# Text scores in half-row groups: two 64-row products at once instead of 128-row products over masked keys

## The chip, the cores and the metric

The kernel runs on one core of a Trainium2 chip. The metric is the device time of one execution in microseconds (µs). Three runs of the kernel before gave 744.82, 745.06 and 745.11, so the median is 745.06. The core has a tensor engine (PE, with its weight loads shown as a row of their own, PEld), a vector engine (DVE), a scalar engine (ACT), a general engine (POOL) and a queue (SP) that issues most transfers. Products are made in single precision; each product shows as two matmul instructions in the profile, each with a weight load.

## The reference

The block is a cross attention with a second, "adapter" attention beside it. Only the first part is touched by the change in the main loop, but both share the tensor engine.

```
query = hidden @ Wq                      # hidden: 2 x 2048 x 640, 8 heads of 80
keyt  = enc @ Wk ; valt = enc @ Wv       # enc: 2 x 124 text tokens x 384
hs    = mha(query, keyt, valt)           # softmax over the 124 tokens, head by head
ca_q1 = einsum('btc,th->bch', ca, Wq_ca)[:, indices]   # 4 adapter tokens
ca_hs1 = mha(ca_q1, hidden, hidden)      # 2048 keys
ca_hs2 = mha(ca_hs1 @ Wq, ca @ Wk_ca, ca @ Wv_ca)
out = (hs + ca_hs2) @ Wout + b_out + hidden
```

## The kernel before, in words

The 2 x 2048 rows are cut into 32 tiles of 128 rows, 16 for each of the two batch entries. Four tiles make a block of 512 rows, for which the queries are made; two tiles make a unit, for which the values and the output are made.

**Features.** Two heads have 160 features together, so a group of two heads does not fit 128 partitions. The kernel keeps queries and keys, both with features on partitions, as five chunks: chunks 0 to 3 hold the first 128 features of each pair of heads (80 of the even head, 48 of the odd one), and chunk 4 holds the remaining 32 of each of the four pairs. `columns` (L390) cuts the columns of a weight matrix this way, for `wq_sb` and for the keys' weights.

**Keys.** `setup_keys` (L584) makes the keys of the text, a chunk at a time (`pk`), and writes them to `kpad`, multiplied by a mask. Each of chunks 0 to 3 is written twice, once with only the even head's features left and once with only the odd head's (`side`); chunk 4 is written four times, once for each pair (`quarter`).

**Scores.** `scores` (L971) makes the text scores of two tiles. For a tile and for each half `u` of the heads (four heads) it takes one PSUM bank `sc` and makes three products over 128 rows, with 248 columns each: two chunks of two heads, and chunk 4 for the two odd heads. DVE takes the maximum of each row and head (`m<-sc`) and subtracts it (`p<-sc`). After each half there is a `yield`, at which other work can be put. When both halves are done, ACT takes the exponential, DVE the sum and its reciprocal, POOL the division (`divided`), DVE turns the result (`eb`), which then goes through memory (`kept`) and comes back as `pT`, with tokens on partitions.

**Values and output.** `values` makes the products `ph` (tokens to features), and `po` (with `Wout`), and DVE adds `po` to the rows.

**The adapter.** Its steps are a main line in the program, twice, once for each batch entry: `maxima` (products `s` of 32 rows with 512 columns, four at once, and a DVE maximum of 2048 elements), `less_maxima` (`pm`), and `contraction` (`s` with 384 columns, ACT's exponential, and `acc`). `yz_block` (`pyz`) and `y_rows` (`pt_y`) prepare their operands. `setup_a2` prepares the adapter's first weights, out of `k2`, `blk["k"]` and the turned `Wq`; `groups_turned` (L464) turns `k2` so that its features lie on partitions.

**Order.** The order of the tensor engine is written out by the program: `TensorInOrder` adds up an estimated time of each product, and `weave` and `Mix` put text work (queries, scores, values) into gaps of the adapter's main line by that estimate. `together` and `beside` take one step of each of several generators in turn, from `yield` to `yield`. The SP queue also keeps the program's order. Other engines take their instructions in the order that the tile framework gives them.

**PSUM.** There are eight banks. The adapter's `s` has four (`sq`) and `acc` one (`ps_a`). Text products take turns in the three of `ps_m`, in the maxima of the second batch entry with `ps_a` as a fourth; only when the adapter is through do they have all eight. A product that takes a bank waits until the reader of the bank's last product is done.

Of the kernel before, what the change touches and what calls it, by code (L numbers as in the profile page):

```python
# [8 lines left out]
F32 = mybir.dt.float32  # L9
# [4 lines left out]
P = 128  # L14
HEADS = 8
T = 4
# [161 lines left out]
def kernel(  # L178
# [129 lines left out]
    band(side2, [[-VH, 2]], VH)  # L308
    eighth = const.tile([P, HEADS], F32, name="eighth")
    band(eighth, [[-VR, HEADS]], VR)  # L310
    s2f = const.tile([P, NCC, HEADS, T], F32, name="s2f")
    nc.gpsimd.memset(s2f, 0.0)

# [7 lines left out]
    wyz4 = const.tile([P, B, 4, G], F32, name="wyz4")  # L321
    nc.gpsimd.memset(wyz, 0.0)
    nc.gpsimd.memset(wyz4, 0.0)
    kpad = const.tile([P, B, 3 * 4, NK], F32, name="kpad")

    vpad = [const.tile([P, HEADS, VH + 2 * VR], F32, name=f"vpad_{b}") for b in range(B)]
    y_sb = const.tile([P, NST, HEADS, G], F32, name="y_sb")
# [61 lines left out]

    def columns(t, last):  # L390

        dve.tensor_copy(
            last.rearrange("p n (g d) -> p n g d", g=4),
            t.rearrange("p n (g d) -> p n g d", g=4)[:, :, :, P:],
        )
        return lambda i, c: t[:, i, D2 * c : D2 * c + P] if c < 4 else last[:, i, :]

    ctxT = sp.tile([P, NCC, B, NTOK], F32, name="ctxT")

# [61 lines left out]
                )  # L461
        return pg

    def groups_turned(name, t, n):  # L464

        pt = mm_tile(name)
        transpose(pt[:, :P], t[:, :P], ident)
        for g in range(4):
            matmul(
                pt[R * g : R * (g + 1), P : P + n], t[:, P:], ident[:, G * g : G * g + n],  # L470
                start=True, stop=True, skip_group_check=True,
            )
        return pt[:, :P].rearrange("p (c k) -> p c k", c=4), pt[:, P : P + n]

    def by_blocks(name, *products):

# [13 lines left out]
    def setup_a2():  # L490

        pg = by_groups("p2_kca", cadT, w_c["kca"])
        k2 = sp.tile([P, D2], F32, name="k2")
        evacuate(k2, pg[:, :D2])
        yield 2.0
        load_w("vca", Wv_ca)

        wqT = []
        for i in range(NCH):
            if i < 4:  # L500
                t = xrow.tile([P, H], F32, tag="x", name=f"wqT_{i}")
            else:
                t = sp.tile([P, H], F32, name=f"wqT_{i}")
            wqT.append(t.rearrange("p (c s) -> p c s", c=NCH))
            for c0, c1 in ((0, 4), (4, NCH)):
                pt = mm_tile(f"pt_wq_{i}_{c0}")
                for c in range(c0, c1):
                    transpose(pt[:, (c - c0) * P : (c - c0 + 1) * P], wq_of(i, c), ident)
                evacuate(
                    wqT[i][:, c0:c1], pt[:, : (c1 - c0) * P].rearrange("p (c s) -> p c s", s=P)  # L510
                )
            yield 1.5
            if i == 0:
                most, rest = groups_turned("pt_k2", k2, B * T1)
                for j in range(2):
                    k0 = T1 * j
                    dve.tensor_scalar(
                        blk["k"][:, 0, :, : B * 2 * T1].rearrange("p c (b k) -> p c b k", b=B)[
                            :, :, :, k0 : k0 + T1
                        ],  # L520
                        most[:, :, : B * T1].rearrange("p c (b t) -> p c b t", b=B),
                        side[:, j : j + 1], None, ALU.mult,
                    )
                dve.tensor_tensor(
                    blk["k"][:, 1, :, : B * 2 * T1].rearrange("p c (b k) -> p c b k", b=B)[
                        :, :, :, T1:
                    ],
                    rest.rearrange("p (x b t) -> p x b t", x=1, b=B).to_broadcast([P, 4, B, T1]),
                    quarter.rearrange("p (g x y) -> p g x y", x=1, y=1).to_broadcast(
                        [P, 4, B, T1]  # L530
                    ),
                    ALU.mult,
                )
                yield 1.5
        a2 = sp.tile([P, NCH * P], F32, name="a2")
        pa = [mm_tile("pa2_0", ps_a), mm_tile("pa2_1")]
        by_blocks(
            "k",
            *[(pa[i // 4][:, i % 4 * P : (i % 4 + 1) * P], lambda c, t=wqT[i]: t[:, c], i % 4 == 0)
              for i in range(NCH)],  # L540
        )
        nc.scalar.copy(a2[:, : 4 * P], pa[0])
        dve.tensor_copy(a2[:, 4 * P :], pa[1][:, :P])
        yield 1.5
        for c0, c1 in ((0, 4), (4, NCH)):
# [38 lines left out]
    def setup_keys():  # L584


        load_w("v", Wv)
        k_of = columns(w_c["k"], sp.tile([P, NCC, P], F32, tag="w4", name="k4"))
        for c in range(NCH):
            pk = mm_tile(f"pk_{c}")  # L590
            for cc in range(NCC):
                matmul(
                    pk[:, : B * NTOK],
                    k_of(cc, c),
                    ctxT[:, cc, :, :].rearrange("p b t -> p (b t)"),
                    start=(cc == 0),
                    stop=(cc == NCC - 1),
                )
            pk3 = pk[:, : B * NTOK].rearrange("p (b t) -> p b t", b=B)[:, :, :NK]
            for i in range(2 if c < 4 else 4):  # L600
                of = side[:, i : i + 1] if c < 4 else quarter[:, i : i + 1]
                dve.tensor_scalar(kpad[:, :, 2 * c + i, :], pk3, of, None, ALU.mult)
            yield
        setup_rows()

# [11 lines left out]
    def setup_values():  # L617
# [21 lines left out]
        for j in range(2):  # L639
# [8 lines left out]
        for b in range(B):  # L648
            n = 2 * T
            dve.tensor_tensor(  # L650
                blk["v"][:, 1, :, n * b : n * (b + 1)].rearrange("p g (j t) -> p g j t", j=2),
                rest[:, T * b : T * (b + 1)].rearrange("p (x y t) -> p x y t", x=1, y=1).to_broadcast(
                    [P, 4, 2, T]
                ),
                eighth.rearrange("p (g j x) -> p g j x", g=4, x=1).to_broadcast([P, 4, 2, T]),
                ALU.mult,
            )
        yield
        for b in range(B):
            nc.gpsimd.memset(vpad[b], 0.0)  # L660
# [310 lines left out]
    def scores(m):  # L971

        q = q_of[m // 2]
        before = None
        for b, st in tiles(m):
            rows = slice(st % 4 * P, (st % 4 + 1) * P)
            e = pools["e"].tile([P, HEADS, NTOK], F32, tag="e", name=f"p_{b}_{st}")
            for u in range(2):
                sc = mm_tile(f"sc_{b}_{st}_{u}")
                for i, c in enumerate((2 * u, 2 * u + 1, 4)):  # L980
                    to = sc[:, : 4 * NK].rearrange("p (i j k) -> p i j k", i=2, j=2)
                    n0 = 2 * c if c < 4 else 2 * (4 + u)
                    matmul(
                        to[:, i, :, :] if c < 4 else to[:, :, 1, :],
                        q[:, c, rows],
                        kpad[:, b, n0 : n0 + 2, :],
                        start=(i == 0),
                        stop=(i == 2),
                        skip_group_check=True,
                    )  # L990
                s4 = sc[:, : 4 * NK].rearrange("p (h k) -> p h k", k=NK)
                m = small.tile([P, 4], F32, tag="m", name=f"m_{b}_{st}_{u}")
                dve.tensor_reduce(m, s4, AX.X, ALU.max)
                dve.tensor_tensor(
                    e[:, 4 * u : 4 * u + 4, :NK], s4,
                    m.unsqueeze(2).to_broadcast([P, 4, NK]), ALU.subtract,
                )
                yield
            nc.scalar.activation(e[:, :, :NK], e[:, :, :NK], AF.Exp, scale=SCALE)  # L999
            nc.gpsimd.memset(e[:, :, NK:], 0.0)  # L1000
            if before is not None:
                divided(*before)
            before = b, st, e
        yield
        divided(*before)
# [343 lines left out]
```

## Time and profile before

| | |
|---|---|
| median of three runs | 745.06 µs (744.82 to 745.11) |
| the profiled execution, first to last instruction | 747.5 µs |
| PE busy | 728.9 µs, 98% |
| DVE busy | 372.4 µs, 50% |
| ACT busy | 197.3 µs, 26% |
| POOL busy | 133.4 µs, 18% |
| granted clock of PE | 1.000 of full speed |

The span of the profiled execution is all the time that the profile tells of it, and is 2.4 µs above the median of the runs. In a group of instructions a form such as 64*128 says how many rows and columns of the tensor engine's array an instruction takes, and 64x512 how many partitions and columns its moving operand has. Busy time is a union: products overlap in the engine, so the time that a product adds is read from the distance between starts of what follows it, not from its own duration.

### The profile page before, as it was taken

The page shows a single profiled execution, that of the slowest core. Times are in us where ns is not written, and L with a number is a line of the kernel's source. Part 1 is how long each engine was busy: PE and PEld are TensorE (multiplying, and loading weights), DVE is VectorE, ACT ScalarE, POOL GpSimd, SP SyncE. Part 2 cuts the span into 40 slices and gives each one's busy share as a digit, 9 for nine tenths or more (in the row PEclk, how much of TensorE's full clock was granted, in tenths as well). Part 3 has the DMA queues.
Part 4 walks back from the last instruction along what each step waited for, and adds up shares of the span by engine and source line. Part 5 has one row for each costly group of instructions (what it writes and reads, how often), then busy time and mean ns, then how long its engine had stood idle before and what let it go on. Part 6 is the DMA issues. An engine that isn't in the chain of part 4 may idle for free.

```text
span 747.5 us, 9397 instructions
## 1 busy us (share of the span) xinstructions
PE 728.9 (98%) x3809; PEld 373.7 (50%) x3809; DVE 372.4 (50%) x500; ACT 197.3 (26%) x246; POOL 133.4 (18%) x184
## 2 busy tenths in 40 slices
PE   6989999999999999999999999999999999999998
PEld 4553443343345455555545454534443556566765
DVE  2046747553164446677768585411340546345631
ACT  2221122024444443212011110443534411011100
POOL 7000000002021012316220220010010012631330
PEclk9999999999999999999999999999999999999999
DMA  9909070005623968499998295410920426985883
GB/s 286 178 3 157 1 71 1 0 1 152 66 92 74 182 115 190 117 260 211 245 177 216 36 191 116 134 33 14 187 54 18 127 92 198 232 218 152 219 241 96
DMA packets 147429, 96.28 MB, mean 129 GB/s; under 512 B 118133, under 2 KB 118965, under 8 KB 145338
## 3 DMA queue, kind: packets, MB, share of 16 engines
q1 hardware_dynamic: 142266, 85.10, 48.1%
q0 software_dynamic: 5120, 10.59, 8.0%
q8 instruction: 30, 0.49, 0.3%
q14 instruction: 13, 0.11, 0.1%
HBM read 63.81 MB, written 31.85 MB: 128 GB/s over the span
## 4 chain that ended last, share of the span: by engine, by line
PE 91%; DVE 4%; DMA 2%; issue 1%; ACT 1%; POOL 0%; SPq 0%; DVEq 0%; ACTq 0%; POOLq 0%
PE pq L28 24%; PE po L28 23%; PE s L28 13%; PE sc L28 11%; PE acc L28 6%; PE ph L28 6%; PE pyz L28 3%; DMA pT<-kept 1%; PE pk L28 1%; PE pv L28 1%; PE pt_y L41 1%; DMA xz<-in_x_dram 1%; ACT ea L856 1%; DVE xt L55 1%; DVE p L55 1%
## 5 line engine op out<-in xcount | busy, mean ns | idle before, releaser
L28 PE MATMUL po<-wout_sb,hsT 128*128 128x320 f32 x640 | 186.5, 438 | 0.6 <-DVE xo L55 0.6
L28 PE MATMUL pq<-xt,wq_sb 128*128 128x512 f32 x320 | 153.7, 612 | 0.0
L28 PEld LDWEIGHTS po<-wout_sb,hsT 128*128 128x128 f32 x640 | 118.5, 190 | 69.6 <-issue 25.1
L55 DVE TENSOR_REDUCE mx<-s 128x4 f32<-128x2048 f32 x48 | 109.9, 2290 | 66.1 <-PE s L28 66.1
L856 ACT ACTIVATE ea<-s 128x1536 f32<-128x1536 f32 x64 | 92.7, 1449 | 106.1 <-PE s L28 106.0
L1014 POOL TENSOR_TENSOR p<-p,r 128x992 f32<-128x992 f32 x32 | 61.6, 1984 | 262.4 <-DVE r L55 262.4
L55 DVE TENSOR_TENSOR xo<-xo,po 128x320 f32<-128x320 f32 x64 | 30.9, 483 | 140.8 <-PE po L28 140.8
L28 PEld LDWEIGHTS pq<-xt,wq_sb 128*128 128x128 f32 x320 | 58.1, 192 | 75.7 <-issue 70.2
L28 PE MATMUL sc<-kpad,q 128*128 128x248 f32 x384 | 94.1, 384 | 0.9 <-DVE p L55 0.9
L28 PEld LDWEIGHTS sc<-kpad,q 128*128 128x128 f32 x384 | 69.2, 189 | 33.7 <-issue 18.5
L55 DVE TENSOR_REDUCE m<-sc 128x4 f32<-128x496 f32 x64 | 42.4, 667 | 62.2 <-PE sc L28 62.2
L272 ACT COPY q<-pq 128x512 f32<-128x512 f32 x31 | 18.2, 586 | 171.0 <-PE pq L28 171.0
L28 PE MATMUL s<-ca,yz 32*128 32x384 f32 x512 | 59.4, 533 | 2.3 <-ACT ea L856 2.3
L999 ACT ACTIVATE p<-p 128x992 f32<-128x992 f32 x32 | 33.0, 1030 | 92.3 <-DVE p L55 92.3
L28 PE MATMUL s<-yz,ca 32*128 32x512 f32 x384 | 54.7, 640 | 1.8 <-DVE mx L55 1.0
L28 PE MATMUL acc<-ea,y_sb 128*32 128x384 f32 x512 | 54.5, 498 | 1.6 <-ACT ea L856 1.6
L1109 POOL DMA_INDIRECT xo<-o,query x24 | 37.4, 1558 | 99.3 <-DMA xo<-in_x_dram 50.7
L28 PE MATMUL ph<-pT,vpad 128*32 128x256 f32 (+1 forms) x512 | 50.0, 387 | 0.2 <-DMA pT<-kept 0.2
L55 DVE TENSOR_TENSOR p<-sc,m 128x496 f32<-128x496 f32 x64 | 42.6, 671 | 1.7
L55 DVE STREAM_TRANSPOSE eb<-p 128x1024 f32<-128x1024 f32 x32 | 38.1, 1223 | 3.6 <-POOL p L1014 3.6
L28 PE MATMUL pq<-xt,wq 128*128 128x512 f32 x80 | 38.3, 603 | 0.0
L55 DVE TENSOR_REDUCE r<-p 128x8 f32<-128x992 f32 (+1 forms) x34 | 37.7, 1111 | 0.0
(142 smaller groups left out, 393.8 us busy)
## 6 DMA issues: line engine op xcount, KB each, us to landing
kept<-eb SPq DMA_DIRECT2D x16, 1024.0 KB, 5.4
pT<-kept SPq DMA_DIRECT2D x64, 256.0 KB, 5.7
xi<-in_x_dram SPq DMA_DIRECT2D x44, 256.0 KB, 5.2
xo<-in_x_dram SPq DMA_DIRECT2D x32, 320.0 KB, 5.3
out_dram<-xo SPq DMA_DIRECT2D x22, 320.0 KB, 2.2
xi<-in_x_dram SPq DMA_DIRECT2D x44, 64.0 KB, 4.2
early<-xo SPq DMA_DIRECT2D x8, 320.0 KB, 2.6
xe<-early SPq DMA_DIRECT2D x8, 320.0 KB, 5.5
```

Source lines behind the costliest of these rows:

```text
L28: ins = self.tc.nc.tensor.matmul(out, lhsT, rhs, **kw)
L41: ins = self.tc.nc.tensor.transpose(out, in_, ident)
L55: self.last = getattr(self.tc.nc.vector, name)(*args, **kw).ins
L272: nc.scalar.copy(dst, src)
L856: nc.scalar.activation(e, q4[:, :, :CAD], AF.Exp, scale=SCALE)
L999: nc.scalar.activation(e[:, :, :NK], e[:, :, :NK], AF.Exp, scale=SCALE)
L1014: nc.gpsimd.tensor_tensor(et, et, r.unsqueeze(2).to_broadcast([P, HEADS, NK]), ALU.mult)
L1109: nc.gpsimd.indirect_dma_start(out=t, out_offset=None, in_=o2_of[b], in_offset=bass.IndirectOffsetOnAxis(ap=query[:, st : st + 1], axis=0) ...
```

## The change

The five chunks are cut anew. Chunk `c` of 0 to 3 now holds the last 64 features of the even head on partitions 0 to 63 and the first 64 of the odd head on partitions 64 to 127; chunk 4 holds, on each half, the remaining 16 features of the four even or of the four odd heads. Keys of chunks 0 to 3 are copied as they are (`kmain`), and those of chunk 4 are written four times with a mask (`krest`, `fourth`).

A tile now takes both banks at once. For each of the four pairs there are two products over 64 rows and 124 columns, one on each half of the partitions and into a bank of its own; then two over 64 rows and 496 columns for the remaining features. Even heads end in one bank, odd heads in the other. There is one `yield` for a tile where there were two. The maxima and differences are the same four DVE instructions per tile. `k2` and its turning follow the new chunks: the transposed remainder is now one product with a spread copy (`wide`) and a folded unit matrix (`fold`), and the masks are written by `spread_rest`, whose lines stood in `setup_values` before.

```diff
+    fourth = const.tile([P, 4], F32, name="fourth")
+    nc.gpsimd.tensor_tensor(fourth, eighth[:, :4], eighth[:, 4:], ALU.add)
...
-    kpad = const.tile([P, B, 3 * 4, NK], F32, name="kpad")
+    kmain = const.tile([P, B, 4, NK], F32, name="kmain")
+    krest = const.tile([P, B, 4, NK], F32, name="krest")
...
     def columns(t, last):
 
-        dve.tensor_copy(
-            last.rearrange("p n (g d) -> p n g d", g=4),
-            t.rearrange("p n (g d) -> p n g d", g=4)[:, :, :, P:],
-        )
-        return lambda i, c: t[:, i, D2 * c : D2 * c + P] if c < 4 else last[:, i, :]
+        pairs = t.rearrange("p n (g d) -> p n g d", g=4)
+        rest = last.rearrange("p n (j g d) -> p n j g d", g=4, j=2)
+        dve.tensor_copy(rest[:, :, 0], pairs[:, :, :, :VR])
+        dve.tensor_copy(rest[:, :, 1], pairs[:, :, :, VR + P :])
+        return lambda i, c: t[:, i, D2 * c + VR : D2 * c + VR + P] if c < 4 else last[:, i, :]
...
-    def groups_turned(name, t, n):
+    def groups_turned(name, t, n, apart=False):
 
         pt = mm_tile(name)
         transpose(pt[:, :P], t[:, :P], ident)
-        for g in range(4):
+        if apart:
+            wide = sp.tile([P, 2, 4, VR], F32, name="wide")
+            dve.tensor_tensor(
+                wide, t[:, P:].rearrange("p (j x d) -> p j x d", j=2, x=1).to_broadcast([P, 2, 4, VR]),
+                quarter.rearrange("p (y g x) -> p y g x", y=1, x=1).to_broadcast([P, 2, 4, VR]),
+                ALU.mult,
+            )
+            fold = sp.tile([P, G], F32, name="fold")
+            dve.tensor_reduce(fold, ident.rearrange("p (g k) -> p k g", k=G), AX.X, ALU.add)
+            matmul(
+                pt[:, P : P + n], wide.rearrange("p j g d -> p (j g d)"), fold[:, :n],
+                start=True, stop=True, skip_group_check=True,
+            )
+        for g in range(0 if apart else 4):
...
-        evacuate(k2, pg[:, :D2])
+        evacuate(k2[:, :P], pg[:, VR : VR + P])
+        evacuate(k2[:, P : P + VR], pg[:, :VR])
+        evacuate(k2[:, P + VR :], pg[:, VR + P : D2])
...
-            for i in range(2 if c < 4 else 4):
-                of = side[:, i : i + 1] if c < 4 else quarter[:, i : i + 1]
-                dve.tensor_scalar(kpad[:, :, 2 * c + i, :], pk3, of, None, ALU.mult)
+            if c < 4:
+                dve.tensor_copy(kmain[:, :, c, :], pk3)
+            for i in range(4 if c == 4 else 0):
+                of = fourth[:, i : i + 1]
+                dve.tensor_scalar(krest[:, :, i, :], pk3, of, None, ALU.mult)
...
+            sc = [mm_tile(f"sc_{b}_{st}_{u}") for u in range(2)]
+            for j in range(4):
+                for u in range(2):
+                    half = slice(VH * u, VH * (u + 1))
+                    matmul(
+                        sc[u][:, j * NK : (j + 1) * NK], q[half, j, rows], kmain[half, b, j, :],
+                        start=(j == 0), stop=False, skip_group_check=True,
+                    )
             for u in range(2):
-                sc = mm_tile(f"sc_{b}_{st}_{u}")
-                for i, c in enumerate((2 * u, 2 * u + 1, 4)):
...
+                half = slice(VH * u, VH * (u + 1))
+                matmul(
+                    sc[u][:, : 4 * NK], q[half, 4, rows],
+                    krest[half, b].rearrange("p j k -> p (j k)"),
+                    start=False, stop=True, skip_group_check=True,
+                )
+            for u in range(2):
+                s4 = sc[u][:, : 4 * NK].rearrange("p (h k) -> p h k", k=NK)
                 m = small.tile([P, 4], F32, tag="m", name=f"m_{b}_{st}_{u}")
                 dve.tensor_reduce(m, s4, AX.X, ALU.max)
                 dve.tensor_tensor(
-                    e[:, 4 * u : 4 * u + 4, :NK], s4,
+                    e.rearrange("p (j u) k -> p j u k", u=2)[:, :, u, :NK], s4,
                     m.unsqueeze(2).to_broadcast([P, 4, NK]), ALU.subtract,
                 )
-                yield
+            yield
```

More of the change, by code (lines that the diff above doesn't have):

```diff
@@ L473, in groups_turned, with spread_rest @@
         return pt[:, :P].rearrange("p (c k) -> p c k", c=4), pt[:, P : P + n]
+    def spread_rest(to, rest, t, own):
+        for b in range(B):
+            n = 2 * t
+            dve.tensor_tensor(
+                to[:, 1, :, n * b : n * (b + 1)].rearrange("p g (j t) -> p g j t", j=2),
+                rest[:, t * b : t * (b + 1)].rearrange("p (x y t) -> p x y t", x=1, y=1).to_broadcast(
+                    [P, 4, 2, t]
+                ),
+                own.to_broadcast([P, 4, 2, t]),
+                ALU.mult,
+            )
     def by_blocks(name, *products):
@@ L513, in setup_a2 @@
             if i == 0:
-                most, rest = groups_turned("pt_k2", k2, B * T1)
+                most, rest = groups_turned("pt_k2", k2, B * T1, True)
                 for j in range(2):
@@ L521, in setup_a2 @@
                         most[:, :, : B * T1].rearrange("p c (b t) -> p c b t", b=B),
-                        side[:, j : j + 1], None, ALU.mult,
+                        side2[:, j : j + 1], None, ALU.mult,
                     )
[L524 to L533, printed above, removed]
+                spread_rest(blk["k"], rest, T1, eighth.rearrange("p (j g x) -> p g j x", g=4, x=1))
                 yield 1.5
@@ L647, in setup_values @@
             )
[L648 to L657, printed above, removed]
+        spread_rest(blk["v"], rest, T, eighth.rearrange("p (g j x) -> p g j x", g=4, x=1))
         yield
@@ L977, in scores @@
             e = pools["e"].tile([P, HEADS, NTOK], F32, tag="e", name=f"p_{b}_{st}")
-            for u in range(2):
-                sc = mm_tile(f"sc_{b}_{st}_{u}")
-                for i, c in enumerate((2 * u, 2 * u + 1, 4)):
[L981 to L991, printed above, removed]
+            sc = [mm_tile(f"sc_{b}_{st}_{u}") for u in range(2)]
[6 more added lines that the diff above has]
+                    )
+            for u in range(2):
+                half = slice(VH * u, VH * (u + 1))
[3 more added lines that the diff above has]
+                    start=False, stop=True, skip_group_check=True,
+                )
+            for u in range(2):
+                s4 = sc[u][:, : 4 * NK].rearrange("p (h k) -> p h k", k=NK)
                 m = small.tile([P, 4], F32, tag="m", name=f"m_{b}_{st}_{u}")
```

## The prediction

> **What bounds the kernel now.** I read the busy times first, then the engines by stretch, the costliest groups, the order of time on PE, and the chain that ended last.
>
> The page and the view by stretches (columns: length, then PE, PEld, DVE, ACT and POOL busy with instructions in brackets):
>
> ```profile
> PE 728.9 (98%) x3809; PEld 373.7 (50%) x3809; DVE 372.4 (50%) x500; ACT 197.3 (26%) x246; POOL 133.4 (18%) x184
> 15.00:55.00 40.00, 37.90 (x201) 20.75 (x203) 9.91 (x29) 8.51 (x19) 0.00 (x0) 1.00 0.53 118
> 290.00:430.00 140.00, 138.56 (x666) 74.63 (x666) 100.80 (x118) 28.34 (x47) 39.21 (x34) 1.00 0.78 180
> 600.00:747.00 147.00, 143.89 (x639) 92.60 (x637) 66.60 (x107) 17.65 (x28) 44.31 (x34) 1.00 0.67 181
> PE 91%; DVE 4%; DMA 2%; issue 1%; ACT 1%; POOL 0%; SPq 0%; DVEq 0%; ACTq 0%; POOLq 0%
> ```
>
> PE is busy in every stretch, at a granted clock of 1.00, and 91% of the chain that ended last is PE. DVE comes nearest to it in one stretch, with 100.8 of 140. So time taken off PE comes off the span, until a wait takes its place.
>
> The groups, every shape apart (busy, mean ns of one, idle before):
>
> ```profile
> L28 PE MATMUL sc<-kpad,q 128*128 128x248 f32 x384 | 94.1, 384 | 0.9 <-DVE p L55 0.9
> L55 DVE TENSOR_TENSOR p<-sc,m 128x496 f32<-128x496 f32 x64 | 42.6, 671 | 1.7
> L55 DVE TENSOR_REDUCE m<-sc 128x4 f32<-128x496 f32 x64 | 42.4, 667 | 62.2 <-PE sc L28 62.2
> L28 PE MATMUL pyz<-xt,wyz 64*128 64x512 f32 x32 | 9.0, 641 | 0.0
> L28 PEld LDWEIGHTS pyz<-xt,wyz 64*128 64x128 f32 x32 | 2.4, 184 | 6.5 <-issue 6.5
> L55 DVE TENSOR_SCALAR kpad<-pk,side 128x248 f32<-128x248 f32 x8 | 3.4, 472 | 15.1 <-PE pk L28 15.1
> ```
>
> The scores are 384 instructions, 12 a tile. The fourth line is the form that the change brings, with 512 columns: two products, one on each half of the rows, as in the changed scores. 32 of them fill 9.0 µs, 0.28 each, though one lasts 0.64.
>
> The order of time on PE (start, length, instruction, count); starts are subtracted below:
>
> ```profile
> 49.17 0.71 PE L41 MATMUL pt_a<-ident,a 128*128 128x128 f32 x5
> 49.71 1.02 PE L28 MATMUL pq<-xt,wq 128*128 128x512 f32 x2
> ...
> 62.80 1.14 PE L28 MATMUL s<-yz,ca 32*128 32x512 f32 x8
> 63.87 2.84 PE L28 MATMUL pq<-xt,wq_sb 128*128 128x512 f32 x6
> 66.64 1.14 PE L28 MATMUL s<-yz,ca 32*128 32x512 f32 x8
> ...
> 673.74 4.46 PE L28 MATMUL pq<-xt,wq 128*128 128x512 f32 x10
> 678.03 2.89 PE L28 MATMUL sc<-kpad,q 128*128 128x248 f32 x12
> 680.85 2.95 PE L28 MATMUL ph<-pT,vpad 128*64 128x256 f32 x32
> 683.73 2.78 PE L28 MATMUL sc<-kpad,q 128*128 128x248 f32 x12
> 686.35 3.93 PE L28 MATMUL po<-wout_sb,hsT 128*128 128x320 f32 x14
> ```
>
> Four prices come from it. **A column:** ten instructions of 512 columns take 678.03 − 673.74 = 4.29, 0.429 each; 124 columns are 0.104 and 496 are 0.416 in proportion. **A change of form:** six such instructions between two `s` take 66.64 − 63.87 = 2.77, 0.20 more than 6 × 0.429; so leaving a form and entering another costs 0.20 (the old products run out, and the first weights load uncovered). **Side by side:** eight `s` instructions take 1.07; less 0.20 that is two passes of 0.43, so the four row groups run at once. **A short pass:** five `pt_a` of 128 columns, each with weights of its own, take 0.54, 0.108 each.
>
> **The change part by part.**
>
> *The products.* An old tile from 683.73 to 686.35 takes 2.62, with the entering half of one change of form; 2.62 − 0.10 = 2.52, 12 × 0.21. A new tile has 10 products, 20 instructions, as pairs on the two halves: 4 pairs × 2 instructions = 8 passes of 124 columns and 2 of 496. I take 0.11 for a short pass, from `pt_a`, since it too loads 128 columns of weights for every pass; the ends are 0.104 (columns alone) and 0.21 (load 0.107, then columns: the load alone is about half of the 0.20). The sum is 8 × 0.11 + 2 × 0.416 = 1.71. It saves 2.51 − 1.71 = 0.80 a tile, 32 × 0.80 = 25.6.
>
> *A rule against the row.* The nearest row, `pt_a`, hides the load of the next weights behind a pass on the same rows, and the second loads of `s` and of the 64-row `pyz` start while their first passes run. The Trainium skill (TensorE: Matmul & The Clock Gate, Part 3, "The mechanism") says that a weight load overlaps with products in flight only when its row group differs; here the next weights go to the same half. By the rule a short pass would be 0.21 and the sum would end at 752 (rival B); by the row it is 0.11. I go by the row.
>
> *Changes of form.* A 64-row tile differs in form from every neighbour but `pyz`. But old tiles came in 56 pieces, mostly between `acc`, `ph` and `s`, which are other forms anyway; new ones come in 29. Counted over the whole order of both programs, stretches of one form go from 375 to 380: 5 × 0.20 = +1.0.
>
> *Banks.* Both banks now fill at the same moment, and DVE needs 0.67 + 0.67 for each. So the first is given back 1.35 after the pair, the second 2.7; before, the first was read while the second filled (1.25). 26 of 32 tiles lie where text work has three or four banks. Laying the new order of PE against 1.35 and 2.7, the next users come too early in four places: after the first tile of all, where `pm` and the second tile follow at once, by 1.2 and 0.9 (before, one place by 0.8), and where `o2` products follow a pair, twice by 0.7. That is 3.5 − 0.8 = +2.7. In about ten more places less than 1.6 is left. In the trace 12 of the 52 maxima in that part start over 0.7 after their product, by 2.2 in the mean, because DVE is in an `eb` or `xt` transpose or the maximum of `s`. Ten places × a quarter × about 1.3 = +3.3. I take +6.0; the ends are +2.7 and +17.4 (rival A).
>
> *One yield for two.* Units of `together` and `beside` now take a tile where they took half. Exponential, sum, division and transposes of a tile stay far ahead of use: `ph` needs them a unit later, 20 to 40 µs. Where the cover is thin is the end. The last `ph` waited for its `pT`:
>
> ```profile
> 722.44 7.57 DMA pT<-kept
> 730.14 2.95 PE L28 MATMUL ph<-pT,vpad 128*64 128x256 f32 x32 [0.17 <-DMA pT<-kept]
> ```
>
> There is one `pT` buffer, so a load can't start before the last `ph` is done. In unit 13 the old order has `ph`, 12 `sc`, 40 `po`, 13.5 for the next load; the new one has both tiles ahead of `ph`, and only 40 `po`, 10.8, remain. The last unit's load already filled 10.8 and 0.2 more. I take +0.5, between 0 and 2.
>
> *Setup.* Twice PE waited 0.50 for a bank of `pk` while DVE scaled it twice (0.47 each); one copy per chunk gives it back 0.47 earlier: −0.9. Against it stand one more DVE copy in each of two `columns`, three short evacuations of `k2` for one, `wide` and `fold` on DVE, and one POOL addition, each a few tenths and beside queries of 0.43 a pass; the turned `k2` is used only after four more rounds of `Wq`'s transposes, some 10 µs later. If that cover were gone they would cost about 1.5. The four small products of `k2` (0.18 together) become one of two passes, nothing to speak of. I take −0.7, between −0.9 and +0.8.
>
> *DVE, ACT, POOL per tile* keep their instructions and sizes; only the stride of what the difference writes changes.
>
> *Sum:* −25.6 + 1.0 + 6.0 + 0.5 − 0.7 = −18.8. Against the span, 747.5 − 18.8 = 728.7. The median of the runs is 2.4 below the span, and I keep that distance: 745.06 − 18.8 = **726.3**.
>
> **The rivals.**
>
> *A: the banks come back late nearly everywhere.* If each of the 26 pairs costs PE one DVE instruction, 0.67, that is 17.4 in place of 6.0: 737.7. For it: `mx` takes 2.29 at a time, and DVE works 72% from 290 to 430. Against it: most pairs are followed by `s` and `acc` of the adapter, 1.7 µs that need no bank of these, and PE waited only 0.9 for `sc` before. It would turn the sign at (18.8 + 6.0) / 26 = 0.95 per pair. The Trainium skill (TensorEngine Tiling (Array Packing), "Gotcha 1: PSUM Pressure") warns of just this for row tiling; no run yet shows its size.
>
> *B: weights aren't hidden.* A short pass takes 0.21: 0.10 × 8 × 32 = 25.6 more, 751.9, slower than before. For it: 20 loads a tile instead of 12, and no row shows a 64-row stream of short passes. Against it: `pt_a`. It decides the sign from 0.11 + 18.8 / 256 = 0.183 for a pass.
>
> *C: the change doesn't do what it says; the halves run one after the other.* 16 × 0.11 + 4 × 0.416 = 3.42 a tile, 1.71 more, 32 times: 781. Against it stand the 64-row `pyz`, 0.28 each where one alone needs 0.429, and that the changed products go to two banks as those do.
>
> **How the numbers follow.** My forecast has 0.82, A 0.10, B 0.05, C 0.02, and 0.01 is left for something that cancels to nothing. The forecast's own range: down to 718 with banks at +2.7, setup at −0.9, the end at 0, a pass at 0.104 (−1.5) and no price for changes of form (−1), rounded down; up to 732 with half of A. To leave out no more than 2 in 10 the range reaches to A: 718 to 737. Differences within 0.2% (1.5 µs) are about what this kernel's runs can't tell from no change. Faster: 0.82 + 0.10, less 0.01 for an A beyond its turning point, 0.91; same 0.01; slower 0.08.
>
> **What would show it.** In the new profile a tile of `sc` should be 20 instructions in 1.9 to 2.0 from its start to the next work (with 0.20 for changing form), and the whole group some 60 busy instead of 94.1. Starts on the two halves should lie together. B would show as 0.21 between short passes, A as idle time of `ph`, `pq`, `po` or `sc` behind DVE's `p`, and the end as a longer wait of `ph` for `pT`. The sum fails if waits for banks or for `pT` grow by ten or more, or if a stage that is now covered by PE turns out to be bound by DVE.

## The result, and the profile after

The changed kernel takes 763.7 µs (median of four runs, 762.22 to 768.17) where the kernel before takes 745.04: a ratio of 1.0255, with an interval of 1.0224 to 1.0286. The forecast was 726.3, faster. The profiled execution has a span of 763.4; its own time is 765.1.

The products did what was forecast. The order of PE in the changed kernel, near its end:

```profile
708.92 1.16 PE L28 MATMUL sc<-kmain,q 64*128 64x124 f32 x16
709.91 1.00 PE L28 MATMUL sc<-krest,q 64*128 64x496 f32 x4
710.75 1.05 PE L28 MATMUL sc<-kmain,q 64*128 64x124 f32 x16
711.64 1.00 PE L28 MATMUL sc<-krest,q 64*128 64x496 f32 x4
712.57 2.95 PE L28 MATMUL ph<-pT,vpad 128*64 128x256 f32 x32
```

Two tiles take 712.57 − 708.92 = 3.65. Less 0.20 for entering and leaving the form that is 1.73 a tile; an old one took 2.51. The starts on the two halves lie 0.006 to 0.007 apart, and from pair to pair of 124 columns it is 0.112. The time was lost elsewhere, as the page of the changed kernel shows (busy times, then the chain that ended last), and with it the groups with every shape apart:

```profile
PE 715.4 (94%) x4059; PEld 345.8 (45%) x4059; DVE 368.5 (48%) x501; ACT 195.5 (26%) x248; POOL 133.1 (17%) x185
PE 78%; DVE 13%; ACT 3%; issue 3%; DMA 2%; POOL 1%; SPq 0%; ACTq 0%; DVEq 0%; POOLq 0%
...
L28 PE MATMUL s<-ca,yz 32*128 32x384 f32 x512 | 60.9, 545 | 22.9 <-ACT ea L871 21.4 <-DVE ca L55 1.4
L28 PE MATMUL sc<-kmain,q 64*128 64x124 f32 x512 | 41.4, 293 | 2.7 <-DVE p L55 1.1 <-ACT o L940 0.7 <-ACT hsT L272 0.7
L28 PE MATMUL sc<-krest,q 64*128 64x496 f32 x128 | 33.9, 586 | 0.0
L1017 ACT ACTIVATE p<-p 128x992 f32<-128x992 f32 x32 | 33.0, 1030 | 145.6 <-DVE p L55 145.6
```

PE is busy for 94% where it was 98, and its share of the chain falls from 91% to 78%, with DVE at 13. The scores are 41.4 + 33.9 busy, 68.0 where the two overlap once, in place of 94.1; the prediction looked for some 60. The large idle time is not in the scores. It stands ahead of the adapter's `s` in the contraction, 22.9 µs, and is put down to ACT's exponential `ea`. The same groups of the kernel before:

```profile
L28 PE MATMUL s<-ca,yz 32*128 32x384 f32 x512 | 59.4, 533 | 2.3 <-ACT ea L856 2.3
L999 ACT ACTIVATE p<-p 128x992 f32<-128x992 f32 x32 | 33.0, 1030 | 92.3 <-DVE p L55 92.3
```

`s` waited 2.3 there. ACT is no busier than before (195.5 against 197.3), but it stands idle ahead of the tile's exponential `p<-p` for 145.6 instead of 92.3, waiting for DVE. By stretches, the loss lies in the two contractions of the adapter, 147 to 280 and 420 to 600 (length, then busy PE, PEld, DVE, ACT, POOL; granted clock; DMA), first the changed kernel, then the one before:

```profile
147.00:280.00 133.00, 120.32 (x831) 49.89 (x823) 57.65 (x84) 51.78 (x44) 15.25 (x14) 0.99 0.39 89
420.00:600.00 180.00, 167.69 (x1043) 74.42 (x1043) 75.99 (x99) 57.90 (x55) 15.72 (x17) 0.98 0.38 94
```

```profile
147.00:280.00 133.00, 129.19 (x790) 59.13 (x789) 58.31 (x85) 54.79 (x45) 15.27 (x14) 1.00 0.48 96
420.00:600.00 180.00, 179.03 (x1040) 83.52 (x1039) 74.81 (x104) 62.32 (x56) 15.15 (x16) 1.00 0.41 94
```

In 313 µs PE is idle 25.0 where it was idle 4.8. DVE is busy for 42 to 43% of them, so it isn't the bound by its amount of work.

**One place, step by step.** This is the order of time on DVE, PE and ACT in the kernel before, around the second half of a tile:

```profile
250.75 1.52 PE L28 MATMUL sc<-kpad,q 128*128 128x248 f32 x6
...
252.20 0.93 PE L28 MATMUL s<-ca,yz 32*128 32x384 f32 x8
252.31 0.67 DVE L55 TENSOR_REDUCE m<-sc 128x4 f32<-128x496 f32 x1 [0.73 <-PE sc L28]
253.02 0.67 DVE L55 TENSOR_TENSOR p<-sc,m 128x496 f32<-128x496 f32 x1
...
253.78 1.03 ACT L999 ACTIVATE p<-p 128x992 f32<-128x992 f32 x1 [3.18 <-DVE p L55]
...
254.72 1.43 ACT L856 ACTIVATE ea<-s 128x1536 f32<-128x1536 f32 x1
...
256.21 0.93 PE L28 MATMUL s<-ca,yz 32*128 32x384 f32 x8 [1.28 <-ACT ea L856]
```

And this is the changed kernel, around a whole tile:

```profile
581.00 2.36 DVE L55 STREAM_TRANSPOSE eb<-p 128x1024 f32<-128x1024 f32 x2
...
582.41 0.93 PE L28 MATMUL s<-ca,yz 32*128 32x384 f32 x8
...
583.28 1.22 DVE L55 TENSOR_REDUCE m<-sc 128x4 f32<-128x496 f32 x2
...
584.42 1.24 DVE L55 TENSOR_TENSOR p<-sc,m 128x496 f32<-128x496 f32 x2
585.76 1.03 ACT L1017 ACTIVATE p<-p 128x992 f32<-128x992 f32 x1 [5.68 <-DVE p L55]
586.69 1.43 ACT L871 ACTIVATE ea<-s 128x1536 f32<-128x1536 f32 x1
...
588.18 1.66 PE L28 MATMUL s<-ca,yz 32*128 32x384 f32 x8 [3.04 <-ACT ea L871]
```

ACT takes its instructions here in the order of its queue. In both listings the tile's exponential `p<-p` stands ahead of the adapter's `ea` in that queue, though the `s` of this `ea` is done long before: at 253.13 in the first listing and 583.34 in the second. `p<-p` needs the differences of the whole tile from DVE, and `ea` waits behind it. The next `s` waits too, because `sq` is one buffer of four banks which `ea` must first read. Before, the first half had been worked by DVE while the second was multiplied. Only two DVE instructions followed the last product, and `ea` came 1.59 late (254.72 − 253.13). Of that 1.28 stayed as a wait here, and all `s` together waited 2.3 (`acc`, which needs the same `ea`, waited 1.6). Now both halves are ready at once, and four DVE instructions, 2.38 here, follow the last product, behind transposes of other tiles (`eb`, to 583.36): `ea` comes 3.35 late, and 3.04 of it stays. I measured this for all 64 `ea` as the distance from the end of the `s` to its start: before, 11 of them are late by 15.2 in all; in the changed kernel 13 by 36.1, most by 2.88 or 3.36. The wait of `s` for them went from 2.3 to 21.4. The likely reason, not shown by itself, is that the products between two `s` cover about as much as before, and the lateness above that is all wait.

**The clock.** After some of these pauses the same products run slower. Windows of the changed kernel, with the granted clock third from the end of the line:

```profile
581.00:585.20 4.20, 4.13 (x40) 1.63 (x37) 4.20 (x7) 0.00 (x0) 0.25 (x2) 1.00 0.46 185
588.20:594.50 6.30, 6.30 (x40) 3.00 (x40) 0.00 (x0) 1.85 (x2) 0.00 (x0) 0.55 0.17 67
```

In the second window eight `s` last 1.66 instead of 0.93. The last section shows after which pauses that happens.

**The sum.** From the first `pyz` (the start before it varies between executions) to the end of the last product PE takes 710.1 against 693.1, 17.0 more. In this stretch of the traces PE stands idle for 39.0 against 8.2. It also works for 12.2 at half the clock against none; half of that time, 6.1, is lost. Together that is 36.9 more. All the rest fell by 19.9, the gain of the new products with their changes of form. Of the 36.9, 19.1 is `s` behind ACT (21.4 less 2.3), 6.1 the lower clock, 5.4 the end, below, and 7.6 other waits, most of them for banks; `acc` behind ACT waits 1.3 less.

### The profile page after: what moved, and what is told of

Its sections match the earlier page's. It is cut to its first block, busy times and chain, and to the rows that moved or that the text cites. A ratio compares the mean times of both kernels' runs of the same rounds, so it can differ in the third digit from the quotient of the medians.

```text
span 763.4 us, 9909 instructions
## 1 busy us (share of the span) xinstructions
PE 715.4 (94%) x4059; PEld 345.8 (45%) x4059; DVE 368.5 (48%) x501; ACT 195.5 (26%) x248; POOL 133.1 (17%) x185
## 4 chain that ended last, share of the span: by engine, by line
PE 78%; DVE 13%; ACT 3%; issue 3%; DMA 2%; POOL 1%; SPq 0%; ACTq 0%; DVEq 0%; POOLq 0%
PE po L28 22%; PE pq L28 22%; PE s L28 12%; PE acc L28 6%; PE sc L28 4%; DVE m L55 4%; DVE p L55 3%; DVE eb L55 3%; PE ph L28 3%; PE pyz L28 3%; ACT ea L871 2%; DMA pT<-kept 1%; DVE mx L55 1%; PE pk L28 1%; PE pv L28 1%
## 5 line engine op out<-in xcount | busy, mean ns | idle before, releaser
L28 PE MATMUL s<-ca,yz 32*128 32x384 f32 x512 | 60.9, 545 | 22.9 <-ACT ea L871 21.4
L1017 ACT ACTIVATE p<-p 128x992 f32<-128x992 f32 x32 | 33.0, 1030 | 145.6 <-DVE p L55 145.6
L55 DVE TENSOR_REDUCE m<-sc 128x4 f32<-128x496 f32 x64 | 41.4, 660 | 52.7 <-PE sc L28 52.7
L28 PE MATMUL acc<-ea,y_sb 128*32 128x384 f32 x512 | 56.5, 514 | 0.3 <-ACT ea L871 0.3
L1127 POOL DMA_INDIRECT xo<-o,query x22 | 34.2, 1556 | 101.0 <-DMA xo<-in_x_dram 56.1
L28 PEld LDWEIGHTS s<-ca,yz 32*128 32x128 f32 x512 | 20.4, 187 | 60.6 <-ACT ea L871 31.4
L28 PEld LDWEIGHTS sc<-kmain,q 64*128 64x128 f32 x512 | 34.8, 196 | 22.2 <-issue 15.9
L1018 POOL MEMSET p<- 128x32 f32 x32 | 5.5, 174 | 224.4 <-DVE eb L55 224.4
L28 PE MATMUL sc<-kmain,q 64*128 64x124 f32 x512 | 41.4, 293 | 2.7 <-DVE p L55 1.1
```

Of the source, the lines that this page charges most:

```text
L28: ins = self.tc.nc.tensor.matmul(out, lhsT, rhs, **kw)
L55: self.last = getattr(self.tc.nc.vector, name)(*args, **kw).ins
L1127: nc.gpsimd.indirect_dma_start(out=t, out_offset=None, in_=o2_of[b], in_offset=bass.IndirectOffsetOnAxis(ap=query[:, st : st + 1], axis=0) ...
```

## The experiments

The theory, Q where a text uses a letter: the order of ACT's queue costs the most, since the later and longer group of DVE instructions now delays the adapter's exponential. Its rivals are that the number of steps per tile is wrong for the order of the program (Y), that the banks come back late (K), that DVE's speed does it, or that the new products themselves do.

### The tile's exponential held behind the adapter's

```diff
-            nc.scalar.activation(e[:, :, :NK], e[:, :, :NK], AF.Exp, scale=SCALE)
+            ex = nc.scalar.activation(e[:, :, :NK], e[:, :, :NK], AF.Exp, scale=SCALE).ins
+            if ea_last:
+                dve.behind(ex, ea_last[0])
...
-                nc.scalar.activation(e, q4[:, :, :CAD], AF.Exp, scale=SCALE)
+                ea_last[:] = [nc.scalar.activation(e, q4[:, :, :CAD], AF.Exp, scale=SCALE).ins]
```

`behind` fixes the order of two instructions on one engine without a wait: `p<-p` may not stand ahead of the last `ea` issued before it. Nothing else changes; the products, banks and yields are the changed kernel's.

> The changed kernel with one thing added: the exponential of a tile may not stand on ACT ahead of an exponential of the adapter that the program issued before it. All computation stays. Theory Q: the waits of s behind ea fall to under 8 and the time to 740 to 750, as far as the order of ACT moves. Rivals K and Y: within 4 of 763.7.

The same order in the kernel before:

> The kernel before, with the exponential of a tile held behind every adapter exponential that the program issued before it. Theory Q: before, the adapter's exponential was late by 15.2 in all, but PE's waits for ACT were only about 5 of it (s 3.3, acc 1.7), so the gain is 2 to 6: 739 to 743. If holding the exponential back helps in another way than by these waits (a better order for DVE or POOL): under 738.

The changed kernel with this order takes 735.3, a ratio to the kernel before of 0.9847 (0.9784 to 0.9909): 28.4 off the changed kernel, faster than the kernel before, and below the 740 to 750 expected. The kernel before gains only 4.3 by it (740.76, ratio 0.9941, 0.9914 to 0.9968). The groups of the changed kernel with the order:

```profile
L28 PE MATMUL s<-ca,yz 32*128 32x384 f32 x512 | 59.4, 533 | 1.4 <-DVE ca L55 1.4
L1017 ACT ACTIVATE p<-p 128x992 f32<-128x992 f32 x32 | 32.9, 1029 | 86.6 <-DVE p L55 86.6
```

No `ea` is late, and `s` doesn't wait for ACT. The edit touches only that order, so this shows what the order costs: 28.4 in the changed kernel, 4.3 before. With the same order in both, the change is worth 740.76 − 735.3 = 5.5 (7.0 by the two ratios, each to runs of the kernel before beside it), not the 18.8 forecast. So the order explains why the sign was wrong, and not the whole distance.

### The exponential that waits for nothing

```diff
-            nc.scalar.activation(e[:, :, :NK], e[:, :, :NK], AF.Exp, scale=SCALE)
+            nc.scalar.activation(idle, idle, AF.Exp, scale=-1.0)
```

The scores' own exponential is left out, and ACT works on an idle tile in its place; the lines are those of the second of two kernels.

> The changed kernel, but the exponential of a tile's scores works on an idle tile of nearly the same size (960 instead of 992 columns) that nothing else writes; so the scores' own exponential is left out, and ACT waits for no DVE instruction there. Theory Q (the queue of ACT: the tile's exponential stands ahead of the adapter's exponential and waits for four DVE instructions, so the adapter's products wait for their bank): the idle time of s behind ea falls from 21.4 to under 4, the pauses of 3 us and the lower granted clock after them go (some 6), and the time falls from 763.7 by about 25, to 736 to 742. Rival K (the text banks come back late, the prediction's rival A): the same banks wait for the same DVE instructions, so within 5 of 763.7. Rival Y (one step per tile makes the order of PE coarser): the order of PE stays, so within 5 of 763.7.

> As the first of these runs (the changed kernel, the scores' own exponential left out, an idle exponential of 960 columns on ACT in its place), but the idle tile lies among the constants and is filled at the start, so that it doesn't make ACT wait for the setup's memory at 115 to 134 us, which cost 10.3 of pauses in the first try. Theory Q: 732 to 737, beside the 735.3 of the pinned exponential. If the first run's pauses were not the filling of the idle tile: 743 to 746 again.

In the first of these the idle tile lay in a late pool. It took 744.55 (ratio 0.9971, 0.9944 to 0.9998), but has two pauses that the changed kernel hasn't:

```profile
114.93 1.98 PE L28 MATMUL pq<-xt,wq_sb 128*128 128x512 f32 x4 [1.77 <-ACT q L272]
134.13 1.97 PE L41 MATMUL pt_y<-ident,yz 128*128 128x128 f32 x8 [8.31 <-ACT yz L790]
```

Some 10 µs come from where that tile was put, so the time, above the 736 to 742 expected, decides nothing. With the tile among the constants it took 740.71 (0.9927, 0.9901 to 0.9952). That is 23 below the changed kernel, as the theory says, though outside the 732 to 737 expected. In its profiled execution the stretch from the first `pyz` to the last product takes 682.0, against 683.1 with the order and 710.1 without; its start took 51.1 where the other took 46.1. Why the start differs stays open.

### DVE's part shortened

The maximum is left out and zeros are subtracted, so that two DVE instructions remain of four.

```diff
-                m = small.tile([P, 4], F32, tag="m", name=f"m_{b}_{st}_{u}")
-                dve.tensor_reduce(m, s4, AX.X, ALU.max)
+                m = zero4
```

> The changed kernel without the maximum over the text scores (a tile of zeros is subtracted in its place, which leaves the stabilising of the softmax out): two DVE instructions per tile are left, as many as stood behind the second half before. Theory Q: the adapter's exponential is late by about 1.5 instead of 2.9 and s waits for it under 6 instead of 21: 738 to 744. Rival K: banks come back at 0.7 and 1.35, 4 to 8 saved, 756 to 760. Rival Y: 760 or more.

It took 743.32 (0.9966, 0.994 to 0.9992). Twelve `ea` are late, most by 1.46, 22.9 in all, against 36.1; and `s` behind ACT falls with it:

```profile
L28 PE MATMUL s<-ca,yz 32*128 32x384 f32 x512 | 60.1, 539 | 13.0 <-ACT ea L873 11.7 <-DVE ca L55 0.8
```

Halving the work that ACT waits for takes 1.4 off most late `ea` and 10 off the wait. The time is inside the 738 to 744 expected, but the wait was expected under 6. Of the 20.4 gained the wait behind ACT has half; other waits fell too, and what each of them is worth isn't told apart here. Changing the order gains more than taking half the work away.

### Is it the new products? The old ones in one step

The kernel before, with both halves of a tile multiplied first, then the four DVE instructions and one `yield`:

```diff
+            scs = []
             for u in range(2):
                 sc = mm_tile(f"sc_{b}_{st}_{u}")
+                scs.append(sc)
...
-                s4 = sc[:, : 4 * NK].rearrange("p (h k) -> p h k", k=NK)
+            for u in range(2):
+                s4 = scs[u][:, : 4 * NK].rearrange("p (h k) -> p h k", k=NK)
...
-                yield
+            yield
```

> The kernel before, its six products of 128 rows, but both halves of a tile are issued in one step, with the four DVE instructions behind them and one yield: the order without the 64-row products. Theory Q: the first half still ends 1.25 ahead of the second, so only two DVE instructions (1.35) are left after the tile, the adapter's exponential is late by 1.6 as before, and the time is 745 to 752. Rival Y: the coarser order costs by itself, 758 or more. Rival K: the second bank comes back 1.4 after the tile instead of 2.7, so 746 to 750.

> The old six products of a tile, both halves first and one yield, with the tile's exponential held behind the adapter's. Unpinned it took 763.1, with s behind ACT 9.1 and waits for banks about 10, where the kernel before had 11.8 of all waits. If the order on ACT is all that one step per tile costs, 745 to 750. If ACT's order has about 6 of it and the banks, filled together with 2.5 of products before DVE may begin, the rest, 755 to 758, s behind ACT under 3 and sc, pm and po behind DVE unchanged at about 10. If neither is the cause, 762 to 764.

The first took 763.1 (1.0212, 1.0151 to 1.0273). That is not the 745 to 752 of the theory; it is what rival Y said, 758 or more. With the order on ACT it took 755.52 (1.0122, 1.0087 to 1.0157), inside the 755 to 758 expected. The groups of the two, in this order:

```profile
L28 PE MATMUL sc<-kpad,q 128*128 128x248 f32 x384 | 87.1, 377 | 4.0 <-DVE p L55 4.0
L28 PE MATMUL s<-ca,yz 32*128 32x384 f32 x512 | 59.4, 533 | 7.6 <-ACT ea L856 7.6
```

```profile
L28 PE MATMUL sc<-kpad,q 128*128 128x248 f32 x384 | 88.0, 380 | 4.0 <-DVE p L55 4.0
L28 PE MATMUL s<-ca,yz 32*128 32x384 f32 x512 | 59.4, 533 | 0.0
```

So taking a tile in one step costs about 18 with the old products too, and with the order set in both kernels it still costs 755.52 − 740.76 = 14.8. Here the queue has only the remaining 3.3 (7.6 with one step, 763.1 − 755.52, less the 4.3 before): for the old products Y is right in the main. By idle time and lower clock the kernel with the order loses 17.5 from the first `pyz` on, the kernel before with the same order 4.1. The largest parts are 4.3 of lower clock (none there), 4.0 of `sc` behind DVE (0.9), 2.9 of `po` (0.6) and 1.1 of the load of `pT` (none). The theory had taken these for nothing. The largest single place is the second half of a tile, which starts only when DVE has taken the difference of the first half, and DVE does two transposes of 1.2 between the maximum and that difference:

```profile
306.50 0.68 DVE L55 TENSOR_REDUCE m<-sc 128x4 f32<-128x496 f32 x1 [1.85 <-PE sc L28]
307.09 2.36 DVE L55 STREAM_TRANSPOSE eb<-p 128x1024 f32<-128x1024 f32 x2
...
309.38 0.64 DVE L55 TENSOR_TENSOR p<-sc,m 128x496 f32<-128x496 f32 x1
...
310.16 2.41 PE L28 MATMUL sc<-kpad,q 128*128 128x248 f32 x6 [3.69 <-DVE p L55]
```

Here too the pause of 3.69 is followed by slow products, 2.41 for what takes 1.42.

### Is it the number of steps?

```diff
             yield
+            yield
             nc.scalar.activation(e[:, :, :NK], e[:, :, :NK], AF.Exp, scale=SCALE)
```

> The changed kernel with a second yield per tile, between the four DVE instructions and the exponential: two steps per tile again, the exponential one step later, nothing held in place. Theory Q: the order of ACT is still free, so some exponentials stand ahead of the adapter's: s waits 6 to 15 instead of 23, time 745 to 757. Rival Y (the number of steps per tile alone makes the difference): the waits for banks and at the end go back to those of before and the time is 730 or less.

It took 786.89 (1.051, 1.0417 to 1.0603), 23 slower than the changed kernel, where the theory had 745 to 757 and Y 730 or less. A second step at this place is no cure: 14 `ea` are late by 39.2 in all, `s` behind ACT rises to 25.5 in the groups, and the mean clock falls to 0.971. The exponential is issued one turn later in the program and still stands ahead of an `ea` in ACT's queue. Only 4 of the 23 are more wait of `s` behind ACT. PE also stands idle longer for other work, and it works for 39.7 at half the clock where the changed kernel has 12.2, which loses some 14 more. With the order set, and with ACT doing the copies out of banks at the end, the second step gave:

> The changed kernel with the exponential held behind the adapter's, the second yield, and, once the adapter is through, copies of queries and values out of PSUM on ACT alone, so that they don't stand behind the DVE instructions of two tiles. Theory Q with the end's own waits (3.6 and its lower clock, 2.5) as measured: 727 to 733.

It took 744.66 (0.998, 0.9951 to 1.0009), above the 727 to 733 expected. `s` doesn't wait for ACT any more, but the tiles now meet readers of banks elsewhere:

```profile
307.21 1.85 PE L28 MATMUL sc<-kmain,q 64*128 64x124 f32 x13 [3.63 <-ACT o L940]
...
339.25 1.87 PE L28 MATMUL sc<-kmain,q 64*128 64x124 f32 x15 [2.70 <-DVE p L55]
```

The same kernel without the second step takes 734.7 (below), so a second step behind the four DVE instructions doesn't help once the queue is right. That is not the second step of the kernel before, which lay between the halves of a tile and with the order set is worth 14.8. No run takes the new products of a tile in two steps, so what that would give stays open, and with it how much of the cost of one step the change could avoid.

### The end

In the changed kernel, after the adapter, the order of PE shows two waits that were 0.17 together:

```profile
718.50 11.04 PE L28 MATMUL po<-wout_sb,hsT 128*128 128x320 f32 x40 [2.97 <-DVE hsT L55]
...
745.80 2.95 PE L28 MATMUL ph<-pT,vpad 128*64 128x256 f32 x32 [2.43 <-DMA pT<-kept]
```

The first is a queue again: two tiles now stand together ahead of `ph`, and DVE's copy of `hsT` comes behind seven of their eight instructions and a transpose. With the order on ACT set, this wait is 3.55, and the 40 `po` after it last 13.59; 40 of them at full clock last 11.03. Two edits of that kernel: the values get the first turn where a unit has no work of the adapter, and the copies at the end all go to ACT.

```diff
-            yield from together(*more, beside(chain(*parts), values(m), 2))
+            yield from together(*more, beside(values(m), chain(*parts), 2))
```

> The changed kernel with the tile's exponential held behind the adapter's, and in units without work of the adapter the values take the first turn, so that the last products of a unit no longer stand behind both tiles of the next scores. In the pinned kernel (735.3) the copy of hsT stands behind eight DVE instructions of two tiles at the end (po behind DVE 3.6 us) and the clock falls after it (about 2.5). If the end is what is left over beyond the order on ACT, this gives 729 (727 to 733), po behind DVE under 1 after 700. If the wait at the end only changes its place (the load of pT, or banks of the tiles, become late instead), it stays at 734 to 738.

```diff
     ps_turns[:] = [ps_m, ps_m, ps_m, ps_a, ps_rest, ps_rest, ps_rest, ps_rest]
+    on[0] = "A"
```

> The changed kernel with the tile's exponential held behind the adapter's, and after the adapter is through the copies out of banks go to ACT alone and not to DVE and ACT in turn. If the wait at the end (po behind DVE hsT 3.6, and about 2.5 of clock after it) comes from the eight DVE instructions of two tiles ahead of that copy, it goes: 729 to 732. If ACT, with exponentials of 1.03 of its own, is no better a place, 734 to 740, with po or ph behind ACT instead.

They took 737.94 (0.9899, 0.9872 to 0.9926) and 734.7 (0.9863, 0.9815 to 0.991), against 735.3: neither is a gain beyond the intervals, and both lie where they were expected if the wait only changes its place. The order of PE near the end, of the first and then of the second:

```profile
682.72 4.58 PE L28 MATMUL ph<-pT,vpad 128*64 128x256 f32 x32 [3.28 <-DMA pT<-kept]
...
718.33 2.95 PE L28 MATMUL ph<-pT,vpad 128*64 128x256 f32 x32 [1.97 <-DMA pT<-kept]
```

```profile
687.06 13.80 PE L28 MATMUL po<-wout_sb,hsT 128*128 128x320 f32 x40 [3.30 <-ACT hsT L272]
```

The wait only changes its place. With the values first, `ph` has too little ahead of it for the load of its `pT`; with ACT, the copy stands behind the tiles' exponentials. Since the kernel with the order alone is the simplest and as fast as any, it is the version to keep: 735.3.

## Why the prediction was wrong, step by step

*The products* were right. 1.73 a tile against 1.71 forecast, 0.112 for a short pass against 0.11. B, which has 0.21, is refuted by these 0.112: the next weights go to the same half of the rows as the products in flight, and their load is hidden all the same. So the rule of the Trainium skill which was set against the row (TensorE: Matmul & The Clock Gate, Part 3, "The mechanism") doesn't hold for this stream. The same section also allows a load into a background weight buffer; no run here shows where a load went. C is refuted by pairs that start 0.006 to 0.007 apart.

*Changes of form* were set too low by a few µs. Their number in the trace hardly moved, 390 to 387, and PE's time without waits and lower clock fell by 19.9 where products and forms together were put at −24.6. The difference lies with the neighbours: 2.3 more at `po` and 1.2 at `pq`, which shared their form with the old tiles and don't with the new; for the rest I have no place.

*Banks* were about as taken: 7.6 of new waits that are neither the queue nor the end, some of them for operands, against +6.0, between the ends of 2.7 and 17.4. The largest place was the one named, the first tile ahead of `pm`, 1.56. So A, as a price of 0.67 for each pair, didn't come. The Trainium skill (TensorEngine Tiling (Array Packing), "Gotcha 1: PSUM Pressure") says only that row tiling raises the pressure on PSUM, and that row tiles write to different banks, not that banks come back late. These waits are what that came to here.

*One yield for two* is the step that failed. It said that "exponential, sum, division and transposes of a tile stay far ahead of use". That held for their own user, `ph`, up to the end, and it was the wrong question. The exponential stands in ACT's queue ahead of another instruction whose user is near, the adapter's `s`, and whether it holds that up depends on when its own input is ready. The same slip is in *DVE, ACT, POOL per tile*: their instructions and sizes did stay, but the moment at which four of them could begin moved. The queue, with the clock that falls after its waits, took 28.4 of the time (763.7 to 735.3), 24.1 more than the 4.3 it took before; no term stood for that, and no rival did. The trace of before had it to be seen: eleven late `ea`, and 92.3 of idle ACT ahead of `p<-p`. What PE waited for ACT there was small, 2.3 at `s` and 1.6 at `acc`.

*The end* was put at +0.5, at most 2, and cost 5.4 (3.2 of `po` behind `hsT` and 2.4 of `ph` behind `pT`, less 0.2). It counted the load of `pT` and not DVE's copy of `hsT`, whose queue had grown by a tile.

*Setup*, put at −0.7, can't be judged: the start varies by 5 or 6 between executions, the first `pyz` coming at 45.3 to 51.2 in the profiled executions of the different kernels.

Between the forecast and the result lie 37.5 (18.7 + 18.8). The queue with its clock has 24.1 of them, the end 4.9, products and forms 4.7, the banks 1.6; some 2 are left. Put together with what was measured, the forecast without its failed step would have been 745.06 − 19.9 + 7.6 = 732.8, and with the end 738.2. The kernel with the order on ACT also sheds the 4.3 that the order was worth before: 733.9, where 735.3 was measured. That they lie so close is partly luck, for its end isn't the same (a wait of 3.55 and a lower clock after it).

## What to carry to other kernels

When a change makes work ready later or all at once, go through each engine that works in order and ask what stands behind the instruction that waits for it, and who needs that; the instruction's own user may be far off and the next one's near. An engine that is 26% busy can hold up the one at 98%. If the order of such a queue is left to a scheduler, fix it by hand before judging a change to the products: the change cost 18.7 with the queue as it came and gained 5.5 with it set in both kernels. And when a change also alters in how many steps the work is handed out, test the steps alone with the old work: here one step for two cost 14.8 by itself, most of what the new products save.

## What the runs showed that was not expected

The granted clock fell after some pauses of PE and not after others, and the length of the pause alone doesn't tell which. In the changed kernel it fell with pauses of 2.56 (ended 252.91), 3.04 (292.64) and 3.04 (588.18), but not with the third pause of 3.04 (527.25) or with 2.97 (718.50). In the kernel with two steps a pause of 2.72 was followed by slow `s`:

```profile
265.42 1.66 PE L28 MATMUL s<-ca,yz 32*128 32x384 f32 x8 [2.72 <-ACT ea L871]
```

The traces show what decides. The clock is full or half, and in each trace all its changes lie on one grid of 3.41 µs; a fall lasts one, two or three steps of it. I took PE's idle time in every step that began at full clock, from 50 µs on, in all thirteen traces. After 30 of these steps the clock fell, and in each of them PE was idle for at least 1.75, about half the step. After 2564 it stayed, and only two of those had more than 1.75 (1.77 and 1.96). So it counts where a pause lies on the grid. The pause of 2.56 put 2.20 into the step from 249.14 to 252.55; that of 3.04 before 527.25 was split into 1.41 and 1.63.

The Trainium skill (TensorE: Matmul & The Clock Gate, Part 1, "What's actually happening") puts the fall to half the clock after an idle window of about 3.4 µs, and says that the window runs freely. The grid of 3.41, which lies elsewhere in each trace, agrees with that; that 1.75 of a window were enough does not, and the measurement decides. So a wait of 3 µs costs up to 6 (3.04, and 0.45 of the 6.3 after 588.20): of the 28.4 that the order gave back, 21.4 was waiting of `s` for ACT and 3.5 lower clock (6.1 to 2.6).
